# Two-layer decoder on one core: layer-norm rows moved to ScalarE, statistics in one tile, slots routing in half steps

## The chip, the core and the metric

The kernel runs on one core of one Trainium2 chip. The metric is the device time of one execution in microseconds, as a median of runs. A core has a TensorE (PE; its weight loads are listed as PEld), a VectorE (DVE), a ScalarE (ACT), a GpSimd (POOL) and a SyncE (SP) that issues most DMAs. Each engine works through its own queue in the order in which the program's scheduler put the instructions.

## What is computed

`x` is 64 sequences (batches) of 128 rows by 256 columns in f32, `ctx` likewise, and `mask` says which rows of a batch are valid. Every step adds to `x` a function of its layer norm:

```python
x = x + L0_attn(ln(x))              # windowed attention, 7 neighbours, 16 heads of 16
x = x + L0_xattn(ln(x), ctx, mask)  # cross attention: (softmax(q k / 4) sm v Wp + bp) * mask
x = x + L0_ffn(ln(x))               # 64 slots: gelu router, top 8, GRU update of the slots
x = x + L1_attn(ln(x))              # causal self-attention with a bias per head (fire)
x = x + L1_xattn(ln(x), ctx)        # cross attention, no mask
x = x + L1_ffn(ln(x))               # quantized linear, depthwise convolution, silu, linear
```

`ln(x)` is `(x - mean) / sqrt(var + 1e-5)` over the columns, without weights. In the first cross attention both the probabilities and the output are multiplied by the row's mask.

## The kernel before

The 64 batches are worked on in 16 groups of `GB` = 4. `x` passes through DRAM between stages; within a stage `Flow.reach(g)` issues the loads of the groups up to g on SP and `Flow.store` writes finished ones back. The stages in the order of time are called A to F here: A window attention (`stage_window`), B the cross attention of layer 0 with the slots feed-forward layer woven in (`stage_cross0`, `Slots`), then the tail of that stage, in which only slots work is left (`slots.finish()`), D self-attention (`stage_attn` with `cross=False` and a bias), E the second cross attention (`stage_attn` with `cross=True`), F the quantized feed-forward layer.

**The layer norm.** `ln_stats` (lines 126 to 137) takes mean and variance of four batches on VectorE (L133, L134), adds 1e-5 (L135, tile `ln_ve`), and raises to the power −0.5 on POOL (L136, `ln_rs`). It has four small tiles: `ln_st`, `ln_mv`, `ln_ve`, `ln_rs`. `layernorm` (L140) then makes the normalized rows on VectorE, one instruction of 128x256 for each batch (L143). Stage A makes its rows on ScalarE instead, by `scaled_rows` (L260): `nm = -mean * rs` on VectorE, then `rs * x + nm` for each batch (L265). `transpose_group` turns rows with PE into two PSUM banks, copied out by ScalarE (L159) and VectorE (L161).

**The attention loop.** `attention_stage` (L577) runs B, D and E. Half step j works on batch n = j // 2 and on half hf = j % 2 of its heads, each a burst of up to 32 score matmuls. In one burst lie the first scores `sm` of batch n (their negated row maxima are wanted) and the second scores `se` of the half step j − 3 (transposed, with the maxima already in the query, for the exponentials). Then:

- `score_halves` (L490): in D the bias is added on VectorE to `sm` (L498, `sb`) and to `se` (L504, `e`); ScalarE takes the exponential (L507, in D L505); VectorE takes the negated maxima (L511, `negmax`).
- even half steps: `shift_query` of the batch begun at j − 2 (PE transposes `negmax`, L523; VectorE adds it to the query, L525, `q`), `divide` of j − 6 (L545 to 556: `rec`, its product with the row mask in B at L554, `ao`), then `prep` of the next batch.
- odd half steps: `weigh_values` of j − 5 (L537, copied by ScalarE to `avs`, L542), `turn_output` of j − 7 (L566, `aT`), `finish_batch` of j − 9 (output projection L176, and the residual sum).
- `tick`, if there is one: a piece of other work.

`sm` and `se` have one PSUM buffer each; the tile `ps`, which everything else of PE writes to, has four.

In B, `prep` (from L672) takes the statistics once a group, and for each batch makes the scaled query rows `qp` on VectorE (L691), adds the masked bias of the output projection to `x` (L694), writes the masked values (`va`, ScalarE), transposes `qp` with PE and copies it out twice on ScalarE into `qt` (L704). The `tick` of B is `Slots.tick`: one step of the routing of a group (`slots_route`, a generator whose `yield`s end the steps) and one step of each of two `slots_update` generators for each group that has been routed. The routing of group g starts after its last batch is finished; its rows `c_xn` come from `layernorm`. What is left when the loop has ended is run by `finish()`.

In D and E, `group_project(g)` is a generator of nine steps (rows `xn`, transposes `xnT`, four halves of query and key, L1142 for the values) which `prep` and `tick` advance, one step in each half step, for the group after the one at work.

Of the kernel before, what the change touches and what calls it, by code (L numbers as in the profile page):

```python
# [10 lines left out]
F = mybir.dt.float32  # L11
# [113 lines left out]

def ln_stats(k, pool, g):
    nc = k.nc
    st = pool.tile([S, GB, 6], F, tag="ln_st", name="ln_st")
    mv = pool.tile([S, GB, 2], F, tag="ln_mv", name="ln_mv")
    ve = pool.tile([S, GB], F, tag="ln_ve", name="ln_ve")  # L130
    rs = pool.tile([S, GB], F, tag="ln_rs", name="ln_rs")
# [3 lines left out]
    nc.vector.tensor_scalar(ve, mv[:, :, 1], 1e-5, None, ALU.add)  # L135
    nc.gpsimd.tensor_tensor(rs, ve, k.expo, ALU.pow)  # L136
    return mv, rs


def layernorm(k, pool, g, out):  # L140
    mv, rs = ln_stats(k, pool, g)
    for b in range(GB):
        k.nc.vector.tensor_scalar(  # L143
            out[:, b, 0:D], k.x[g][:, b, :], mv[:, b, 0:1], rs[:, b : b + 1],
            ALU.subtract, ALU.mult,
        )

# [111 lines left out]

def scaled_rows(k, pool, g, mv, rs, out):  # L260

    nm = pool.tile([S, GB], F, tag="ln_nm", name="ln_nm")
    k.nc.vector.scalar_tensor_tensor(nm, mv[:, :, 0], -1.0, rs, ALU.mult, ALU.mult)
    for b in range(GB):
# [178 lines left out]
class Batch:  # L443
    pass

# [130 lines left out]

def attention_stage(k, pool, w1, prep, wo, lay, bias_s=None, bias_t=None, tick=None):  # L577

# [59 lines left out]
def stage_cross0(k, w, wc):  # L638
# [3 lines left out]
    with k.tc.tile_pool(name="wb", bufs=2) as wp, k.tc.tile_pool(name="wb1", bufs=1) as w1, \  # L642
# [31 lines left out]
        def prep(bi):  # L674
            g, b = divmod(bi, GB)
            if b == 0:
# [5 lines left out]
                nc.vector.tensor_scalar(r4, rs, 0.25, None, ALU.mult)  # L682
                stats[g] = mv, r4
            mv, r4 = stats[g]
            mk = w.mask[:, bi : bi + 1]
            if b == GB - 1 and g + 1 < k.G:
# [7 lines left out]
            nc.vector.scalar_tensor_tensor(xb, w.bp, mk, xb, ALU.mult, ALU.add)  # L694
            cv = cxs[g][:, b, :].rearrange("p (h d) -> p h d", d=DH)
# [3 lines left out]
            t.kt = kts[g % 2][:, :, b * S : (b + 1) * S]  # L699
            p = psum(k)  # L700
            for c in range(2):
                nc.tensor.transpose(p[:, c * S : (c + 1) * S], qp[:, c * 128 : (c + 1) * 128], k.ident)
            for par in range(2):
                nc.scalar.activation(  # L704
                    t.qt[:, par::2], p[:, 0 : 2 * S].rearrange("p (c l) -> p c l", l=S), AF.Identity,
                    scale=w.par[:, par : par + 1], bias=w.row[:, par : par + 1],
                )
            t.va, t.row_scale = va, mk

            def fin(y):  # L710
                nc.vector.scalar_tensor_tensor(xb, y, mk, xb, ALU.mult, ALU.add)

            t.fin = fin
# [18 lines left out]
def prep_cross0(k, pool):  # L732
# [3 lines left out]
    w.bp = load_row(k, pool, "b_bp")  # L736
    w.mask = load(k, pool, "mask")
    w.par = pool.tile([128, 2], F, name="b_par")
    w.row = pool.tile([128, 2], F, name="b_row")
# [351 lines left out]
def stage_attn(k, w, cross, bias=None):  # L1091
# [3 lines left out]
    with k.tc.tile_pool(name=pre, bufs=2) as wp, k.tc.tile_pool(name=pre + "1", bufs=1) as w1:  # L1095
# [8 lines left out]
        def group_project(g):  # L1104

            xn = w1.tile([S, GB, D], F, tag="xn", name="xn")
            kvT = None
            if cross:
                kvT = wp.tile([128, 2, GB * S], F, tag="kvT", name="kvT")
                nc.sync.dma_start(out=kvT, in_=k.a["ctxT"][g])  # L1110
            k.flow.reach(g + 1)
            layernorm(k, wp, g, xn)
            nc.vector.tensor_tensor(
                k.x[g], k.x[g], w.bvo.unsqueeze(1).to_broadcast([S, GB, D]), ALU.add
            )
# [3 lines left out]
            if not cross:  # L1119
                kvT = xnT  # L1120
            yield
# [33 lines left out]
        def advance(g, parts):  # L1155
            for _ in range(parts):
                if g in pending and next(pending[g], pending) is pending:
                    del pending[g]

        def prep(bi):  # L1160
            g, b = divmod(bi, GB)
            if bi == 0:
                pending[0] = group_project(0)
# [8 lines left out]
            t.va, t.row_scale = va[:, b], None  # L1172
            xb = k.x[g][:, b, :]
# [442 lines left out]
```

## Time and profile before

| | us |
|---|---|
| median of three runs | 3199.1 (3198.59 to 3200.51) |
| the profiled execution, its own time | 3198.04 |
| its span in the trace | 3196.2 |
| PE busy in the span | 2756.9 (86%) |
| VectorE busy | 2457.0 (77%) |
| ScalarE busy | 1464.5 (46%) |
| POOL busy | 460.1 (14%) |
| mean granted clock of TensorE | 0.927 |

A row of the profile's tables reads: line of the kernel, engine, operation, the tile written and the tiles read, shape and count; then busy time and the mean of one in ns, and the idle time of the engine just before such instructions with what ended most of it. A timeline row starts with the start in us and the duration; in brackets stands the idle time before it and its releaser. A row of the table of windows gives, for a stretch of the span, its length, the busy time (and instructions) of PE, PEld, DVE, ACT and POOL, the granted clock of TensorE as a share of full speed, the share of the DMA engines that is busy and GB/s. A busy PE is not PE at full speed: the records lengthen when the granted clock is low.

The chain that ended last belongs to PE for 52% of the span and to VectorE for 35%. A score matmul takes 295 ns in the mean (6144 rows of `sm`, 514.1 us), `negmax` 1219 ns, the exponential 1022 ns, `q` 681 ns.

### The profile page before, as it was taken

To read this page: it belongs to the slowest core of one execution; us is meant where nothing else is said; L and a number is where in the kernel's file an instruction comes from. 1 tells how busy PE (TensorE), PEld (TensorE's weight loads), DVE (VectorE), ACT (ScalarE), POOL (GpSimd) and SP (SyncE) were. 2 spreads that over 40 slices of the span, in tenths; PEclk is the share of its full clock that TensorE was granted. 3 is DMA by queue.
4 is the path that set the end of the run, shared out by engine and by line. 5 is a ranking of instruction groups with operands and counts; after the bars stand their busy time and mean duration, and the time that the engine had idled before them with its cause. 6 is when DMAs were issued, how large, how long until landed. Compare 5 with 4: busy or idle time off the path is not lost.

```text
span 3196.2 us, 63468 instructions
## 1 busy us (share of the span) xinstructions
PE 2756.9 (86%) x26850; PEld 1801.7 (56%) x26876; DVE 2457.0 (77%) x4818; ACT 1464.5 (46%) x2395; POOL 460.1 (14%) x360
## 2 busy tenths in 40 slices
PE   5859988688888888888888988979999998888887
PEld 2324433466666666556666666657667775343343
DVE  7967988787777777778888888865655555899997
ACT  3222221264554554434434444435555555766664
POOL 6555764100000000010000000020000000100000
PEclk9968998799999999989989998989999999999998
DMA  4100111211111111000000000011111111010000
GB/s 150 53 16 27 40 40 40 74 37 45 52 42 45 52 35 35 27 29 15 28 28 28 15 28 28 28 47 35 54 41 41 48 48 41 14 35 32 33 20 27
DMA packets 60011, 123.82 MB, mean 39 GB/s; under 512 B 9088, under 2 KB 34064, under 8 KB 59472
## 3 DMA queue, kind: packets, MB, share of 16 engines
q1 hardware_dynamic: 59168, 118.28, 10.8%
q8 instruction: 212, 3.47, 0.4%
q0 software_dynamic: 560, 1.49, 0.2%
q14 instruction: 71, 0.58, 0.1%
HBM read 77.76 MB, written 41.98 MB: 37 GB/s over the span
## 4 chain that ended last, share of the span: by engine, by line
PE 52%; DVE 35%; ACT 4%; issue 4%; POOL 3%; DMA 1%; SPq 0%; DVEq 0%; POOLq 0%; ACTq 0%
PE ps L176 9%; PE ps L167 8%; PE sm L484 8%; PE ps L537 6%; PE se L484 5%; DVE negmax L511 5%; DVE e L504 3%; PE cv L1316 3%; PE ps L1142 3%; DVE hs L1370 2%; DVE pv L372 2%; PE ps L566 2%; DVE hp L1306 2%; DVE oT L376 2%; PE sc L366 1%
## 5 line engine op out<-in xcount | busy, mean ns | idle before, releaser
L484 PE MATMUL sm<-kt,qt 32*128 32x128 f32 x6144 | 514.1, 295 | 113.3 <-DVE negmax L511 95.7
L484 PEld LDWEIGHTS sm<-kt,qt 32*128 32x128 f32 x6144 | 422.2, 192 | 287.1 <-DVE negmax L511 112.4
L484 PE MATMUL se<-q,kt 32*128 32x128 f32 x6144 | 469.2, 292 | 44.7 <-DVE q L525 41.6
L511 DVE TENSOR_REDUCE negmax<-sm 128x8 f32<-128x1024 f32 x256 | 312.0, 1219 | 200.4 <-PE se L484 190.5
L484 PEld LDWEIGHTS se<-q,kt 32*128 32x128 f32 x6144 | 394.1, 194 | 77.5 <-DVE q L525 47.3
L507 ACT ACTIVATE e<-se 128x1024 f32<-128x1024 f32 x256 | 261.6, 1022 | 204.6 <-PE se L484 201.3
L136 POOL TENSOR_TENSOR ln_rs<-ln_ve,expo 128x4 f32<-128x4 f32 x96 | 100.6, 1048 | 1410.5 <-DVE ln_ve L135 1230.8
L1316 PE MATMUL cv<-hp,taps 128*128 128x512 f32 x480 | 241.3, 639 | 35.8 <-DVE hp L1306 35.5
L314 POOL TENSOR_TENSOR pr<-pad,qt 128x896 f32<-128x896 f32 x128 | 247.1, 1953 | 140.6 <-PE s L326 97.2
L505 ACT ACTIVATE e<-e 128x1024 f32<-128x1024 f32 x128 | 135.3, 1057 | 210.4 <-DVE e L504 210.3
L498 DVE TENSOR_TENSOR sb<-sm,bias_s 128x1024 f32<-128x1024 f32 x128 | 153.9, 1202 | 85.8 <-PE se L484 82.0
L542 ACT COPY avs<-ps 128x512 f32<-128x512 f32 x192 | 112.2, 585 | 146.0 <-PE ps L537 145.8
L1316 PEld LDWEIGHTS cv<-hp,taps 128*128 128x128 f32 x480 | 93.3, 203 | 140.4 <-issue 84.0
L372 DVE TENSOR_TENSOR pv<-sc,pad 128x896 f32<-128x896 f32 x128 | 137.8, 1081 | 40.3 <-PE sc L366 40.3
L504 DVE TENSOR_TENSOR e<-se,bias_t 128x1024 f32<-128x1024 f32 x128 | 155.6, 1215 | 3.2 <-PE se L484 1.8
L511 DVE TENSOR_REDUCE negmax<-sb 128x8 f32<-128x1024 f32 x128 | 154.9, 1210 | 0.5
L133 DVE BATCH_NORM_STATS2 ln_st<-x 128x6 f32<-128x256 f32 x384 | 147.6, 427 | 4.4 <-DMA x<-in_x_dram 1.7
L376 DVE TENSOR_REDUCE oT<-pv 128x128 f32<-128x896 f32 x128 | 136.7, 1072 | 1.3
L366 PE MATMUL sc<-fw,spread 32*128 32x448 f32 x512 | 103.5, 649 | 33.4 <-DVE pv L372 28.8
L525 DVE TENSOR_TENSOR q<-ps,qt 128x512 f32<-128x512 f32 x192 | 130.7, 681 | 1.0 <-PE ps L523 1.0
L1176 DVE TENSOR_TENSOR x<-ps,x 128x256 f32<-128x256 f32 x128 | 53.9, 421 | 91.2 <-PE ps L176 91.2
L549 PE MATMUL ps<-ident,avs 128*128 128x128 f32 x768 | 115.5, 273 | 0.7 <-ACT avs L542 0.7
(329 smaller groups left out, 5657.4 us busy)
## 6 DMA issues: line engine op xcount, KB each, us to landing
x<-in_x_dram SPq DMA_DIRECT2D x16, 512.0 KB
ab<-x SPq DMA_DIRECT2D x16, 512.0 KB
x<-ab SPq DMA_DIRECT2D x16, 512.0 KB
cx<-in_ctx_dram SPq DMA_DIRECT2D x16, 512.0 KB
kt<-in_ctxT_dram SPq DMA_DIRECT2D x128, 64.0 KB
cd<-x SPq DMA_DIRECT2D x16, 512.0 KB
x<-cd SPq DMA_DIRECT2D x16, 512.0 KB
de<-x SPq DMA_DIRECT2D x16, 512.0 KB
```

The source lines that it names most:

```text
L167: k.nc.tensor.matmul(out, w[:, kc, c0 : c0 + cn], rhsT[:, kc, n0 : n0 + n], start=(kc == 0), stop=(kc == 1),)
L176: k.nc.tensor.matmul(out, aT[:, kc, :], w[:, kc, :], start=(kc == 0), stop=(kc == 1))
L314: k.nc.gpsimd.tensor_tensor(pr[:, c], shift_windows(t.kt, b, c), t.qt[:, c, b, :].unsqueeze(1).to_broadcast([128, WIN, S]), ALU.mult,)
L372: nc.vector.tensor_tensor(pv, bc[th][:, :, 0 : WIN * 64].rearrange("p c (l w) -> p c l w", w=WIN), shift_windows2(t.vt, b, th), ALU.mult,)
L376: nc.vector.tensor_reduce(oT[:, :, 64 * th : 64 * th + 64], pv, AX.X, ALU.add)
L484: k.nc.tensor.matmul(ts[side][:, rr, c * S : (c + 1) * S], st[rows, c, :], mv[rows, c, :], start=True, stop=True,)
L498: nc.vector.tensor_tensor(sb, src, bias_s[:, hf * 2 : hf * 2 + 2, :], ALU.add)
L504: nc.vector.tensor_tensor(e, est, bias_t[:, hf * 2 : hf * 2 + 2, :], ALU.add)
L507: nc.scalar.activation(e, est, AF.Exp)
L511: nc.vector.tensor_reduce(b.lay.extra(b.nm, hf * 2), src.rearrange("p r (c m) -> p r c m", m=S), AX.X, ALU.max, negate=True,)
L537: nc.tensor.matmul(av[32 * r : 32 * r + 32, c * S : (c + 1) * S], b.va[:, b.lay.head(c, r), :], b.e[r // 2][:, r % 2, c * S : (c + 1) * S] ...
L1316: nc.tensor.matmul(pc, w.taps[:, CONV_PE.index(j), t, :], hp[:, :, t : t + S], start=(t == 0), stop=(t == 2),)
```

## The change

1. *One tile of statistics a group.* `ln_stats` keeps everything in one tile `ln` of ten rows.
2. *Rows on ScalarE.* In B (`qp`), in the slots routing (`c_xn`), and in D and E (`xn`), the normalized rows are made on ScalarE by `activation(Identity, scale, bias)` with `nm` from the new `row_bias`. `layernorm` is gone. D and E also copy both halves of `xnT` on ScalarE.
3. *Slots rows in two half steps.* `slots_route` makes `c_xn` in two steps of two batches each, so it has two `yield`s more.
4. *B's order.* The masked bias, the transposes of `qp` and `qt` become `more()`, called at the end of the odd half step. The output is finished at a lag of 8 half steps instead of 9, ahead of the other parts of its half step. The two factors of the mask (on `rec` and on the output) become one factor `mask * mask` in `fin`.
5. *D's order.* With a bias, `shift_query` stands between the burst and `score_halves`, where it stood behind them.
6. *Groups of D and E begin earlier.* `begin(g + 2)` at the end of the odd half step ahead of a group's first batch; the statistics are the step that `begin` runs, the rows another. The output bias is added to `x` after the transposes. `kvT` (the context in E) has three buffers.

```diff
 def ln_stats(k, pool, g):
+    ln = pool.tile([S, 10, GB], F, tag="ln", name="ln")
+    st = ln[:, 0:6].rearrange("p i b -> p b i")
+    mv = ln[:, 6:8].rearrange("p i b -> p b i")
+    ve, rs = ln[:, 8], ln[:, 9]
...
-def scaled_rows(k, pool, g, mv, rs, out):
+def row_bias(k, pool, mv, rs):
     nm = pool.tile([S, GB], F, tag="ln_nm", name="ln_nm")
     k.nc.vector.scalar_tensor_tensor(nm, mv[:, :, 0], -1.0, rs, ALU.mult, ALU.mult)
-    for b in range(GB):
+    return nm
+
+def scaled_rows(k, pool, g, mv, rs, out, nm=None, bs=range(GB)):
+    if nm is None:
+        nm = row_bias(k, pool, mv, rs)
+    for b in bs:
...
 def divide(k, pool, b):
-    if b.row_scale is not None:
-        nc.vector.tensor_scalar(rec, rec, b.row_scale, None, ALU.mult)
...
 def attention_stage(..., tick=None, lag=9):
+    early = bias_s is not None
     start(0)
+    if bs[0].more:
+        bs[0].more()
...
             ts = score_burst(k, first, second)
+            if early and at(j, 2):
+                shift_query(k, pool, at(j, 2))
             score_halves(k, pool, w1, ts, first, second, bias_s, bias_t)
+        if lag % 2 == hf and at(j, lag):
+            finish_batch(k, bs.pop((j - lag) // 2), wo)
         if hf == 0:
-            if at(j, 2):
+            if not early and at(j, 2):
                 shift_query(k, pool, at(j, 2))
...
-            if at(j, 9):
-                finish_batch(k, bs.pop((j - 9) // 2), wo)
+            if n + 1 < k.NB and bs[n + 1].more:
+                bs[n + 1].more()
...
 # stage_cross0, prep
-                stats[g] = mv, r4
+                stats[g] = r4, row_bias(k, wp, mv, r4)
...
-            nc.vector.tensor_scalar(
-                qp, xb, mv[:, b, 0:1], r4[:, b : b + 1], ALU.subtract, ALU.mult,
+            nc.scalar.activation(
+                qp, xb, AF.Identity, scale=r4[:, b : b + 1], bias=nm[:, b : b + 1]
             )
...
-        attention_stage(k, wp, w1, prep, w.wp, Heads(True), tick=slots.tick)
+        attention_stage(k, wp, w1, prep, w.wp, Heads(True), tick=slots.tick, lag=8)
...
 def slots_route(k, w, g, wp, w1):
-    layernorm(k, wp, g, xn)
-    yield
+    mv, rs = ln_stats(k, wp, g)
+    yield
+    nm = row_bias(k, wp, mv, rs)
+    for half in range(2):
+        scaled_rows(k, wp, g, mv, rs, xn, nm, range(2 * half, 2 * half + 2))
+        yield
...
 # stage_attn, group_project
-            xn = w1.tile([S, GB, D], F, tag="xn", name="xn")
...
-                kvT = wp.tile([128, 2, GB * S], F, tag="kvT", name="kvT")
+                kvT = wp.tile([128, 2, GB * S], F, tag="kvT", name="kvT", bufs=3)
...
-            layernorm(k, wp, g, xn)
+            mv, rs = ln_stats(k, w1, g)
+            yield
+            xn = w1.tile([S, GB, D], F, tag="xn", name="xn")
+            scaled_rows(k, wp, g, mv, rs, xn)
+            yield
+            xnT = w1.tile([128, 2, GB * S], F, tag="xnT", name="xnT")
...
+                nc.scalar.copy(xnT[:, kc, :], p)
...
             nc.vector.tensor_tensor(
                 k.x[g], k.x[g], w.bvo.unsqueeze(1).to_broadcast([S, GB, D]), ALU.add
             )
-            yield
-            xnT = w1.tile([128, 2, GB * S], F, tag="xnT", name="xnT")
-            transpose_group(k, xn, xnT)
...
 # stage_attn, prep and tick
+        def begin(g):
+            if g < k.G and g not in pending:
+                pending[g] = group_project(g)
+                advance(g, 1)
...
-                if g + 1 < k.G:
-                    pending[g + 1] = group_project(g + 1)
+                begin(g + 1)
...
-                advance((j // 2 + 1) // GB + 1, 1)
+                g, b = divmod(j // 2 + 1, GB)
+                advance(g + 1, 1)
+                if b == GB - 1:
+                    begin(g + 2)
```

More of the change, by code (lines that the diff above doesn't have):

```diff
@@ L127, in ln_stats @@
     nc = k.nc
[L128 to L131, printed above, removed]
+    ln = pool.tile([S, 10, GB], F, tag="ln", name="ln")
+    st = ln[:, 0:6].rearrange("p i b -> p b i")
+    mv = ln[:, 6:8].rearrange("p i b -> p b i")
+    ve, rs = ln[:, 8], ln[:, 9]
     for b in range(GB):
@@ L137, in ln_stats @@
     return mv, rs
-def layernorm(k, pool, g, out):
-    mv, rs = ln_stats(k, pool, g)
-    for b in range(GB):
[L143 to L146, printed above, removed]
 def transpose_group(k, src, dst):
@@ L257, in prep_window @@
     return w
-def scaled_rows(k, pool, g, mv, rs, out):
+def row_bias(k, pool, mv, rs):
     nm = pool.tile([S, GB], F, tag="ln_nm", name="ln_nm")
     k.nc.vector.scalar_tensor_tensor(nm, mv[:, :, 0], -1.0, rs, ALU.mult, ALU.mult)
-    for b in range(GB):
+    return nm
[3 more added lines that the diff above has]
+    for b in bs:
         k.nc.scalar.activation(
@@ L443 @@
 class Batch:
-    pass
+    more = None
 class Heads:
@@ L574, in finish_batch, with attention_stage @@
     b.fin(py[:, 0:D])
-def attention_stage(k, pool, w1, prep, wo, lay, bias_s=None, bias_t=None, tick=None):
+def attention_stage(k, pool, w1, prep, wo, lay, bias_s=None, bias_t=None, tick=None, lag=9):
     nms = []
@@ L682, in prep @@
                 nc.vector.tensor_scalar(r4, rs, 0.25, None, ALU.mult)
-                stats[g] = mv, r4
-            mv, r4 = stats[g]
+                stats[g] = r4, row_bias(k, wp, mv, r4)
+            r4, nm = stats[g]
             mk = w.mask[:, bi : bi + 1]
@@ L690, in prep @@
             qp = wp.tile([S, D], F, tag="qp", name="qp")
-            nc.vector.tensor_scalar(
-                qp, xb, mv[:, b, 0:1], r4[:, b : b + 1], ALU.subtract, ALU.mult,
+            nc.scalar.activation(
+                qp, xb, AF.Identity, scale=r4[:, b : b + 1], bias=nm[:, b : b + 1]
             )
-            nc.vector.scalar_tensor_tensor(xb, w.bp, mk, xb, ALU.mult, ALU.add)
             cv = cxs[g][:, b, :].rearrange("p (h d) -> p h d", d=DH)
@@ L699, in prep, with more, fin @@
             t.kt = kts[g % 2][:, :, b * S : (b + 1) * S]
[L700 to L706, printed above, removed]
-                )
[L708 to L713, printed above, removed]
+            t.va = va
+            def more():
+                nc.vector.scalar_tensor_tensor(xb, w.bp, mk, xb, ALU.mult, ALU.add)
+                p = psum(k)
+                for c in range(2):
+                    nc.tensor.transpose(
+                        p[:, c * S : (c + 1) * S], qp[:, c * 128 : (c + 1) * 128], k.ident
+                    )
+                for par in range(2):
+                    nc.scalar.activation(
+                        t.qt[:, par::2], p[:, 0 : 2 * S].rearrange("p (c l) -> p c l", l=S),
+                        AF.Identity, scale=w.par[:, par : par + 1], bias=w.row[:, par : par + 1],
+                    )
+            def fin(y):
+                nc.vector.scalar_tensor_tensor(
+                    xb, y, w.mask2[:, bi : bi + 1], xb, ALU.mult, ALU.add
+                )
+            t.more, t.fin = more, fin
             return t
         slots = Slots(k, wc, c2, w1)
-        attention_stage(k, wp, w1, prep, w.wp, Heads(True), tick=slots.tick)
+        attention_stage(k, wp, w1, prep, w.wp, Heads(True), tick=slots.tick, lag=8)
         slots.finish()
@@ L737, in prep_cross0 @@
     w.mask = load(k, pool, "mask")
+    w.mask2 = pool.tile([S, k.NB], F, name="mask2")
+    nc.vector.tensor_tensor(w.mask2, w.mask, w.mask, ALU.mult)
     w.par = pool.tile([128, 2], F, name="b_par")
@@ L1104, in group_project @@
         def group_project(g):
-            xn = w1.tile([S, GB, D], F, tag="xn", name="xn")
             kvT = None
             if cross:
-                kvT = wp.tile([128, 2, GB * S], F, tag="kvT", name="kvT")
+                kvT = wp.tile([128, 2, GB * S], F, tag="kvT", name="kvT", bufs=3)
                 nc.sync.dma_start(out=kvT, in_=k.a["ctxT"][g])
             k.flow.reach(g + 1)
-            layernorm(k, wp, g, xn)
+            mv, rs = ln_stats(k, w1, g)
[4 more added lines that the diff above has]
+            xnT = w1.tile([128, 2, GB * S], F, tag="xnT", name="xnT")
+            for kc in range(2):
+                p = psum(k)
+                for b in range(GB):
+                    nc.tensor.transpose(
+                        p[:, b * S : (b + 1) * S], xn[:, b, kc * 128 : (kc + 1) * 128], k.ident
+                    )
+                nc.scalar.copy(xnT[:, kc, :], p)
+            if not cross:
+                kvT = xnT
             nc.vector.tensor_tensor(
@@ L1115, in group_project @@
             )
-            yield
-            xnT = w1.tile([128, 2, GB * S], F, tag="xnT", name="xnT")
-            transpose_group(k, xn, xnT)
-            if not cross:
-                kvT = xnT
             yield
@@ L1162, in prep @@
             if bi == 0:
-                pending[0] = group_project(0)
+                begin(0)
             if b == 0:
                 advance(g, 9)
-                if g + 1 < k.G:
-                    pending[g + 1] = group_project(g + 1)
+                begin(g + 1)
             advance(g + 1, 1)
@@ L1171, in prep @@
             t.qt, t.kt = qt[:, :, b * S : (b + 1) * S], kt[:, :, b * S : (b + 1) * S]
-            t.va, t.row_scale = va[:, b], None
+            t.va = va[:, b]
             xb = k.x[g][:, b, :]
```

## The prediction

> **What bounds the kernel now.** I read the table of windows first, cut at the six stages (A window attention, B cross attention of layer 0 with the slots routing between its steps, then B's tail of slots work, D self-attention with bias, E cross attention of layer 1, F bitnet).
>
> ```profile
> core 0: us, PE busy (x) PEld busy (x) DVE busy (x) ACT busy (x) POOL busy (x), PEclk, DMA share, GB/s
> 0.00:593.00 593.00, 471.43 (x2104) 208.73 (x2104) 481.85 (x748) 138.59 (x238) 341.98 (x220) 0.87 0.16 53
> 593.00:1303.00 710.00, 624.12 (x7792) 480.92 (x7792) 542.53 (x1492) 373.68 (x635) 29.76 (x42) 0.92 0.14 44
> 1303.00:1401.00 98.00, 77.35 (x418) 48.92 (x418) 62.39 (x204) 35.68 (x62) 10.79 (x13) 0.86 0.12 41
> 1401.00:2143.00 742.00, 650.64 (x7571) 477.70 (x7570) 610.89 (x881) 309.43 (x466) 30.74 (x41) 0.94 0.07 26
> 2143.00:2690.00 547.00, 526.71 (x7385) 382.89 (x7385) 316.85 (x561) 285.86 (x444) 12.08 (x12) 0.99 0.13 43
> 2690.00:3196.20 506.20, 406.69 (x1594) 202.53 (x1616) 442.45 (x936) 321.25 (x552) 34.71 (x32) 0.93 0.08 29
> ```
>
> PE is busy 86 to 88% of B and D and 96% of E; ScalarE is half idle in all three. VectorE holds 76% of B and 82% of D. So B and D are two engines handing work back and forth, E is PE alone. The spacing of equal rows gives the steady group of four batches: B 47.8 us, D 44.1, E 35.1. In B the timeline of VectorE shows what one group loses at its seam:
>
> ```profile
> 1019.91 0.17 DVE L135 TENSOR_SCALAR ln_ve<-ln_mv 128x4 f32<-128x4 f32 x1
> 1021.27 1.38 DVE L143 TENSOR_SCALAR c_xn<-x,ln_mv,ln_rs 128x256 f32<-128x256 f32 x4 [1.19 <-POOL ln_rs L136]
> 1022.57 1.22 DVE L511 TENSOR_REDUCE negmax<-sm 128x8 f32<-128x1024 f32 x1
> 1023.71 0.68 DVE L525 TENSOR_TENSOR q<-ps,qt 128x512 f32<-128x512 f32 x1
> ```
>
> negmax, which the next burst needs, stands behind a wait of 1.19 us for POOL's power and four c_xn rows (1.38). PE then stands still for 2.71 us, and the windows show what follows: 0.16 us of work, then half clock.
>
> ```profile
> 1022.00:1024.00 2.00, 0.16 (x2) 0.16 (x2) 2.00 (x5) 0.24 (x1) 0.00 (x0) 0.92 0.00 0
> 1024.00:1026.00 2.00, 2.00 (x11) 1.77 (x12) 1.94 (x10) 0.07 (x1) 0.00 (x0) 0.50 0.00 0
> 1026.00:1028.00 2.00, 2.00 (x16) 1.67 (x16) 0.36 (x1) 0.99 (x2) 0.00 (x0) 0.50 0.00 0
> ```
>
> It lasts 6.8 us (1023.7 to 1030.5), 3.4 us of PE's work, in every steady group. In D the timeline of PE shows the other loss, a score burst cut in two by the shifted query:
>
> ```profile
> 1723.13 1.16 PE L484 MATMUL sm<-kt,qt 32*128 32x128 f32 x16
> 1724.86 1.16 PE L484 MATMUL se<-q,kt 32*128 32x128 f32 x16 [0.57 <-DVE q L525]
> ```
>
> Sixteen rows alone take 1.16 us; all 32 interleaved take 1.17 (2392.01 to 2393.19 in E). A cut costs 1.16, and 0.57 of waiting where q is late. In the issue order of the old kernel every odd burst of D is cut; in the new one a quarter, since shift_query goes ahead of the score halves and q no longer stands behind sb, e and negmax of the next step.
>
> **Part by part.** The sum is made against the profiled execution (3198.0 us; span 3196.2), which is 1.1 below the median of 3199.1.
>
> *A, one tile of statistics:* the next group's statistics wait for the whole tile, and nm follows the power at once, so VectorE may wait for POOL there; on POOL's queue the power now stands behind two pr (L314, 1.95 us each). A steady wait has the row above, 1.19 us; 16 groups give 0 to +19, and earlier statistics could give −5. PE (79%) and VectorE (81%) alternate and hide part: **+5**.
>
> *B, ScalarE rows.* Off VectorE per group: four c_xn (0.409 each), four qp (0.363), four products of rec and mask (0.225, L554): 4.0 of a sum of 43.1. Onto ScalarE: eight rows of 0.597 (L265): 27.6 becomes 32.4 of 47.8, so there is room. On the path goes only the seam: 1.19 + 1.38 = 2.57 us ahead of negmax, and the 3.4 us of clock behind it. Two nm (0.17) lie in waits; mask squared is one operation ahead of the stage.
>
> *B, "more".* bp's addition, two transposes and two qt (L704, 0.56 each on ScalarE) move from the even half step to the end of the odd one. Now the next burst needs qt, which stands behind exp, avs and aT on ScalarE. The trace has no such wait. Its ends: 0, where slots work on PE (pieces of 0.75 to 1.8 us) lies between, and transposes 0.27 + exp 1.02 + qt 1.12 = 2.4 us a batch. With exp half done I take 1.4; in the issue order one batch in six has no piece: 4/6 × 1.4 = +0.9 a group. finish a half step earlier (lag 8) puts q behind x (0.42, L1176) in places; PE has the transposes there: 0, at worst 4 × 0.4 a group. Sum −2.6 − 3.4 + 0.9 = −5.0 a group, × 13 steady groups = **−65** (ends −110, all seams and 3.5 of VectorE's 4.0 gone, and +96, below).
>
> *Half steps of slots.* c_xn takes two further ticks: a group's routing takes 9 where there are 8 half steps a group. It falls behind, and one group more is left after the last burst. The tail writes x at 1333.10, 1355.97 and 1378.17, 22.5 apart: **+22.5** (ends 0, if D's projection begins beside it, and +45).
>
> *D.* Per pair of half steps 12.0, 10.41, 10.42, 11.3. Three whole bursts instead of cut ones bring about 1.0 each in two pairs and 0.8 in the others (of 1.73: the rest goes where VectorE is the limit). xn (4 × 0.409) and the xnT copy (0.687) leave VectorE in the last pair; nm and its wait (0.17 + 1.19) come in the first: 12.6, 9.4, 9.4, 8.2 = 39.6. Behind the waiting nm stand the next sb, e and negmax on VectorE, and PE's burst waits for these. A second way: VectorE's sum of 41.3 − 2.3 + 0.2 + 1.2 waiting = 40.4. I take 40.4: −3.7 × 15 = **−56** (ends −100, when the half-clock stretches go as well: windows at 0.5 or less add up to 96 us of D, 48 of work; and −20, if each group gets a new one like B's, 3.4 us of work, a third of it hidden). Here ScalarE's rows lie in its 55% of idle time; without it they would cost 3.1 a group.
>
> *E.* The same move takes out one PE wait of 1.17 + 0.21 us a group, and half the groups show half clock after it:
>
> ```profile
> 2420.00:2422.00 2.00, 0.68 (x3) 0.29 (x2) 2.00 (x8) 0.00 (x0) 0.00 (x0) 1.00 0.78 260
> 2424.00:2426.00 2.00, 2.00 (x28) 1.48 (x17) 1.16 (x2) 1.20 (x3) 0.00 (x0) 0.50 0.00 0
> ```
>
> Together up to 2.2 us a group; exp now stands behind the rows (2.4 us), covered by transposes, avs and Wq on PE. I take 1.6 × 15 = **−24** (0 to −33). Groups begin a half step earlier: the x and context loads move up on SP, past the stores of the group before, and the third context buffer keeps them from waiting for the last reader; at a DMA share of 0.13 I cost that at 0 and, uncovered, one load a group. F changes only in order: **0** (±6).
>
> Sum: 5 − 65 + 22.5 − 56 − 24 = −117: **3081 us**.
>
> *A rule beside the row.* The Trainium skill, "TensorE: Matmul & The Clock Gate", Part 1, says that the array's clock halves after at least one idle window of about 3.4 us, counted freely. This trace differs: the half clock in B follows 2.71 us of idling, in E 1.38. By the page such gaps cost no clock, the 3.4 us a group would have another cause and stay, and the sum would be the first rival's time; the measurement decides against it as far as 13 alike groups can.
>
> **Rivals.**
> 1. *The clock loss stays.* If the half clock after the seam goes with the group's load and not with the idle 2.71 us, B gains 1.6 a group: −21 in place of −65, 3125 us. Against it: it begins right behind the gap, every 47.8 us. For it: dips in A and F without that seam.
> 2. *qt eats B's gain.* At 1.4 us in nearly every batch (+4.7 more a group) B stands still: 3146 us. For it: ScalarE's queue before qt is exp, avs, aT.
> 3. *Slower.* In B the stalls ahead of the burst come in every batch (4 × 1.4) and two of four are long enough to halve the clock (2 × 3.4): −5.0 + 12.4 = +7.4 a group, +96: 3198 − 52.5 + 96 = 3242 us. It decides from +4.0 a group, where D's and E's gains are used up. E's 1.38 us of idling shows that short gaps can do it; against it speaks slots work on PE in five batches of six.
> 4. *D doesn't do what it says:* q comes late, as the sb of the next step waits for its burst and q for the transposes; bursts interleave but wait 1 us longer. D unchanged: 3137 us. For it: q is late by 0.57 us already now; against it: the transposes stand ahead of sb in the new issue order.
> 5. *More goes than I count:* with VectorE's cuts the half-clock stretches of B (89 us) and D go too. For it: most start behind a PE wait for VectorE; against it: E's 1.38 us shows how little it takes. D to −100, B to −110, E to −33: 3198 + 27.5 − 243 = 2982 us.
>
> **Numbers.** Forecast 0.45, rivals 0.15, 0.12, 0.10, 0.09, 0.09. Leaving out the slower case and most of the last gives 2990 to 3170. Faster by over 0.2% (6.4 us, about what a measurement of this kernel can tell) 0.88, within it 0.02, slower 0.10.
>
> **What would show it.** Right: no half clock every group in B, group 42 to 44; negmax with no c_xn ahead; D groups near 40 with three of four odd bursts whole; a wait of about 1.2 us for the power ahead of nm; a tail of about 120 us; E below 34. Wrong: PE waits for ScalarE's qt ahead of most of B's bursts, D at 44 with PE waiting for q, a tail still near 98, or A longer by over 15 us.

## The result, and the profile after

The changed kernel takes 3181.4 us (median of 4 runs, 3176.8 to 3183.7) against 3198.9 of before: a ratio of 0.9942, 95% interval 0.9925 to 0.996. It is faster, as forecast, but by 0.6%: the medians differ by 18 us in place of the forecast 117. The forecast of 3081 us and its range (2990 to 3170) are both missed.

To compare stages I cut both traces at the same events: A ends with the first row maxima of B, then come the last of B, the first of D, the first of E and the last of E. The half-clock column adds the time at a granted clock of 0.5 or less (in brackets: stretches), the idle column the time without a PE row.

| stage | before | after | change | forecast | half clock before, after | PE idle before, after |
|---|---|---|---|---|---|---|
| A | 598.5 | 617.6 | +19.1 | +5 | 165 (17), 177 (19) | 123.8, 133.3 |
| B | 704.4 | 669.2 | −35.2 | −65 | 104 (13), 90 (14) | 83.6, 69.7 |
| tail | 100.7 | 133.5 | +32.8 | +22.5 | 27 (4), 41 (7) | 20.9, 26.2 |
| D | 739.1 | 687.3 | −51.8 | −56 | 96 (18), 75 (14) | 91.1, 65.2 |
| E | 542.2 | 554.6 | +12.4 | −24 | 10 (3), 31 (9) | 20.2, 23.5 |
| F | 511.1 | 512.6 | +1.5 | 0 | 66 (13), 68 (14) | 99.6, 97.8 |

The changes sum to −21.2 us; the profiled spans (3196.2 and 3174.8) differ by 21.4, the rest is rounding. The table of windows of the changed kernel, with these cuts:

```profile
core 0: us, PE busy (x) PEld busy (x) DVE busy (x) ACT busy (x) POOL busy (x), PEclk, DMA share, GB/s
0.00:617.60 617.60, 484.31 (x2124) 215.22 (x2124) 493.34 (x775) 142.57 (x246) 343.46 (x222) 0.86 0.16 53
617.60:1286.90 669.30, 599.57 (x7702) 457.88 (x7703) 473.54 (x1244) 412.62 (x727) 28.53 (x39) 0.93 0.14 43
1286.90:1420.30 133.40, 107.26 (x509) 66.38 (x507) 73.41 (x244) 58.27 (x106) 8.96 (x13) 0.85 0.12 41
1420.30:2107.60 687.30, 622.09 (x7550) 446.76 (x7550) 581.61 (x816) 341.84 (x541) 30.75 (x41) 0.95 0.08 29
2107.60:2662.20 554.60, 531.14 (x7313) 378.08 (x7314) 285.40 (x517) 319.68 (x511) 13.09 (x13) 0.97 0.12 40
```

VectorE lost 102 us of busy time over the whole span (2457.0 to 2355.3) and ScalarE gained 135, as intended; the span followed by a fifth of that. The first hint of where the rest went is what VectorE now waits for. Some of its waits over the whole changed kernel (total, times, longest):

```profile
DVE ln_nm L256 <- POOL ln L138: 89.1, 61, 9.2
DVE x L709 <- ACT qp L698: 80.1, 36, 4.9
DVE x L1147 <- ACT xn L265: 68.1, 18, 7.9
```

nm waits for POOL's power. That wait is not new, but it has grown: ahead of everything that uses the power, VectorE waited 67 us in the kernel before and waits 104 now. The last two are new kinds of wait: the masked bias of B, added to `x` in place, waits until ScalarE has read that `x` for qp; the output bias of D and E waits for ScalarE's xn in the same way. E shows most plainly what such a wait does. VectorE at a seam of the changed E:

```profile
2240.90 1.23 DVE L511 TENSOR_REDUCE negmax<-sm 128x8 f32<-128x1024 f32 x1 [0.56 <-PE se L484]
2245.80 1.22 DVE L1147 TENSOR_TENSOR x<-x,e_bvo 128x1024 f32<-128x1024 f32 x1 [3.68 <-ACT xn L265]
2246.94 1.22 DVE L511 TENSOR_REDUCE negmax<-sm 128x8 f32<-128x1024 f32 x1
```

and ScalarE beside it:

```profile
2242.73 1.07 ACT L1144 COPY xnT<-ps 128x512 f32<-128x512 f32 x2
2243.69 2.08 ACT L265 ACTIVATE xn<-x,ln_nm,ln 128x256 f32<-128x256 f32 x4
```

The burst that this negmax reads ends at 2244.24. VectorE is idle then, but the next in its queue is the bias, which waits until the fourth row of xn ends at 2245.77 and then takes 1.22 us. negmax starts 2.7 us after its data were there, and PE waits for it 1.46 us where it waited 1.17 before. In the kernel before, VectorE has the rows, the same bias and the averages there, with no wait between them:

```profile
2417.29 1.37 DVE L143 TENSOR_SCALAR xn<-x,ln_mv,ln_rs 128x256 f32<-128x256 f32 x4
2418.69 1.23 DVE L1113 TENSOR_TENSOR x<-x,e_bvo 128x1024 f32<-128x1024 f32 x1
2419.84 0.37 DVE L134 BATCH_NORM_AGGREGATE ln_mv<-ln_st 128x2 f32<-128x6 f32 x4
2420.13 1.19 DVE L511 TENSOR_REDUCE negmax<-sm 128x8 f32<-128x1024 f32 x1
```

The xn that left VectorE (1.37 us) was replaced by a wait of 1.5 us for the same xn on ScalarE (2244.24 to 2245.77), and the bias's own 1.22 us stayed. In the changed kernel half clock follows:

```profile
2248.00:2250.00 2.00, 1.58 (x32) 1.30 (x32) 2.00 (x8) 1.15 (x2) 0.00 (x0) 1.00 0.00 0
2250.00:2252.00 2.00, 2.00 (x11) 1.17 (x12) 1.04 (x6) 1.21 (x2) 0.75 (x1) 0.54 0.00 0
```

### The profile page after: what moved, and what is told of

Its sections match the earlier page's. It is cut to its first block, busy times and chain, and to the rows that moved or that the text cites. A ratio compares the mean times of both kernels' runs of the same rounds, so it can differ in the third digit from the quotient of the medians.

```text
span 3174.8 us, 63554 instructions
## 1 busy us (share of the span) xinstructions
PE 2759.1 (87%) x26876; PEld 1769.7 (56%) x26876; DVE 2355.3 (74%) x4531; ACT 1599.2 (50%) x2683; POOL 459.3 (14%) x360
## 4 chain that ended last, share of the span: by engine, by line
PE 48%; DVE 35%; ACT 9%; POOL 4%; issue 2%; DMA 2%; SPq 0%; POOLq 0%; DVEq 0%; ACTq 0%
PE ps L169 9%; PE sm L484 8%; PE ps L160 8%; PE se L484 4%; PE ps L537 4%; DVE negmax L511 3%; PE ps L1171 3%; DVE sb L498 3%; DVE e L504 3%; PE cv L1352 3%; DVE pv L372 2%; DVE hs L1406 2%; DVE oT L376 2%; DVE hp L1342 2%; DVE ln L135 2%
## 5 line engine op out<-in xcount | busy, mean ns | idle before, releaser
L484 PE MATMUL sm<-kt,qt 32*128 32x128 f32 x6144 | 539.3, 297 | 69.2 <-DVE negmax L511 40.2
L484 PEld LDWEIGHTS sm<-kt,qt 32*128 32x128 f32 x6144 | 436.4, 192 | 240.6 <-DVE negmax L511 71.8
L484 PE MATMUL se<-q,kt 32*128 32x128 f32 x6144 | 481.0, 292 | 56.5 <-DVE e L504 25.8
L484 PEld LDWEIGHTS se<-q,kt 32*128 32x128 f32 x6144 | 402.4, 192 | 84.1 <-issue 37.4
L138 POOL TENSOR_TENSOR ln<-ln,expo 128x4 f32<-128x4 f32 x96 | 98.4, 1025 | 1676.2 <-DVE ln L137 1158.8
L314 POOL TENSOR_TENSOR pr<-pad,qt 128x896 f32<-128x896 f32 x128 | 248.4, 1964 | 137.7 <-PE s L326 97.8
L135 DVE BATCH_NORM_STATS2 ln<-x 128x6 f32<-128x256 f32 x384 | 148.8, 406 | 10.9 <-DMA x<-ab 10.5
L265 ACT ACTIVATE xn<-x,ln_nm,ln 128x256 f32<-128x256 f32 x192 | 100.3, 595 | 31.4 <-DVE ln_nm L256 24.7
```

The costliest lines, as they stand in the source:

```text
L314: k.nc.gpsimd.tensor_tensor(pr[:, c], shift_windows(t.kt, b, c), t.qt[:, c, b, :].unsqueeze(1).to_broadcast([128, WIN, S]), ALU.mult,)
L484: k.nc.tensor.matmul(ts[side][:, rr, c * S : (c + 1) * S], st[rows, c, :], mv[rows, c, :], start=True, stop=True,)
```

## The experiments

The theory (theory 1 in the expectations): rows that went to ScalarE turned later operations of VectorE into waits for ScalarE, and these stand at the head of VectorE's queue, ahead of the row maxima that PE needs; with the wait of nm for POOL they ate the gain. The rival: ScalarE's own longer queue delays exp and qt, and VectorE's idle time is only where that shows. A third suspect for A alone was the one tile of statistics.

Each run's stages were cut as above; times in us. The last column is the median of the run's timings, not the profiled span. The kernel before, timed beside each run, had medians of 3198.9 to 3208.8, so that a total is read to about 10 us unless its ratio is given; stages come from the traces, one profiled execution of each run.

| run | A | B | tail | D | E | time |
|---|---|---|---|---|---|---|
| before | 598.5 | 704.4 | 100.7 | 739.1 | 542.2 | 3198.9 |
| changed | 617.6 | 669.2 | 133.5 | 687.3 | 554.6 | 3181.4 |
| x1 four tiles | 603.7 | 671.8 | 131.1 | 654.5 | 558.4 | 3133.7 |
| x2 bias off VectorE's queue | 616.9 | 665.0 | 135.6 | 661.5 | 551.0 | 3141.5 |
| x3 x2 and two buffers | 622.5 | 668.4 | 136.2 | 660.5 | 547.4 | 3149.5 |
| x4 slots rows in one step | 622.4 | 717.9 | 98.9 | 692.5 | 558.3 | 3202.1 |
| x5 x1 and x2 | 606.0 | 661.6 | 132.9 | 650.6 | 524.2 | 3089.4 |
| x6 order undone | 621.2 | 648.8 | 133.6 | 735.3 | 554.5 | 3208.1 |
| x7 x5, E's rows on VectorE | 602.1 | 668.1 | 132.1 | 650.8 | 578.6 | 3148.8 |
| x8 x5, nm on POOL | 598.1 | 667.7 | 133.3 | 654.4 | 526.8 | 3093.1 |
| x9 x5, qt early again | 603.9 | 639.7 | 133.2 | 651.2 | 524.3 | 3068.3 |
| x10 x9, eight half steps | 606.2 | 660.5 | 109.6 | 651.2 | 524.3 | 3060.1 |
| x11 before, one tile alone | 616.8 | 708.0 | 100.6 | 739.2 | 548.1 | 3228.6 |
| x12 before, early query alone | 599.9 | 704.4 | 100.7 | 691.4 | 542.2 | 3152.7 |

Runs whose code is the same in a stage still differ there by up to 6 us in A (the changed kernel, x2 and x3: 616.9 to 622.5) and by 6.5 in B (x5 and x7); in D (x5, x7, x9, x10) and E (x5, x9, x10) by under 1. Differences below that are not read.

### x1: four tiles of statistics again

```diff
 def ln_stats(k, pool, g):
-    ln = pool.tile([S, 10, GB], F, tag="ln", name="ln")
...
+    st = pool.tile([S, GB, 6], F, tag="ln_st", name="ln_st")
+    mv = pool.tile([S, GB, 2], F, tag="ln_mv", name="ln_mv")
+    ve = pool.tile([S, GB], F, tag="ln_ve", name="ln_ve")
+    rs = pool.tile([S, GB], F, tag="ln_rs", name="ln_rs")
```

> The changed kernel with the four small tiles of statistics of before (everything else as changed). Stage A took 598.5 us before and 617.6 after (start to the first negmax of B). If the one tile is what costs A its 19 us, since nm then waits for the power right behind the statistics (1.13 us and more a group), A comes back to 598 to 603. If A lost them to something else (order of weight preparation, clock), it stays above 612. D (687) and E (555) are expected within 5 us of the changed kernel by the first theory, as the waits for ScalarE's rows that I hold responsible there do not come from this tile.

A came back to 603.7, about as expected, but D fell by 33 us, which I had not expected. In the changed D the statistics of a group run in one piece, and nm waits at the end of it:

```profile
1672.39 0.31 DVE L136 BATCH_NORM_AGGREGATE ln<-ln 128x2 f32<-128x6 f32 x2
1672.73 0.17 DVE L137 TENSOR_SCALAR ln<-ln 128x4 f32<-128x4 f32 x1
1674.11 0.16 DVE L256 SCALAR_TENSOR_TENSOR ln_nm<-ln 128x4 f32<-128x4 f32 x1 [1.21 <-POOL ln L138]
1674.19 1.22 DVE L498 TENSOR_TENSOR sb<-sm,bias_s 128x1024 f32<-128x1024 f32 x1
1675.32 0.68 DVE L525 TENSOR_TENSOR q<-ps,qt 128x512 f32<-128x512 f32 x1
```

With four tiles the scheduler lays the parts of two groups over each other: nm of one group stands ahead of the averages of the next, so its power is long done, and no bracket appears.

```profile
1642.13 0.15 DVE L256 SCALAR_TENSOR_TENSOR ln_nm<-ln_mv,ln_rs 128x4 f32<-128x4 f32 x1
...
1645.92 0.37 DVE L136 BATCH_NORM_AGGREGATE ln_mv<-ln_st 128x2 f32<-128x6 f32 x4
1646.33 0.17 DVE L137 TENSOR_SCALAR ln_ve<-ln_mv 128x4 f32<-128x4 f32 x1
1646.40 1.40 DVE L135 BATCH_NORM_STATS2 ln_st<-x 128x6 f32<-128x256 f32 x4
```

PE's wait for sb in D falls with it. First the changed kernel, then x1:

```profile
PE sm L484 <- DVE sb L498: 24.8, 18, 1.7
```

```profile
PE sm L484 <- DVE sb L498: 6.5, 14, 1.6
```

### x11: the one tile alone, in the kernel before

The same edit turned round: the kernel before with the tile `ln` in place of the four.

> The kernel before with the one tile of statistics alone. If one tile keeps the scheduler from spreading a group's statistics over time (its parts can't belong to two groups at once), A 598 becomes 610 to 620, and D (739) and E (542), where VectorE's rows then follow the power at once, grow by 1.2 us a group, 10 to 25 each; the kernel is slower than before by 30 to 60 in all. Rival (the tile costs only where nm follows it on VectorE and ScalarE reads it): A as above, B, D and E within 6 of before.

3228.6 us, a ratio to before of 1.0079 (1.0059 to 1.0099): slower. A 616.8 is the changed kernel's A, so the tile is all of A's 19 us; VectorE's wait ahead of nm in A is 29.3 us in both, against 15.2 before. D did not move, E grew by 6, and B's 4 are within what equal code shows: neither of the two expectations as a whole. So D pays for the tile only together with other parts of the change. The trace above points to nm on VectorE behind the power; no run has the one tile in the changed kernel with nm elsewhere.

### x2 and x3: the biases out of VectorE's queue

```diff
 # group_project (D and E)
-            nc.vector.tensor_tensor(
+            nc.gpsimd.tensor_tensor(
                 k.x[g], k.x[g], w.bvo.unsqueeze(1).to_broadcast([S, GB, D]), ALU.add
 # prep of B
             def more():
-                nc.vector.scalar_tensor_tensor(xb, w.bp, mk, xb, ALU.mult, ALU.add)
...
             def fin(y):
...
+                nc.vector.scalar_tensor_tensor(xb, w.bp, mk, xb, ALU.mult, ALU.add)
 # x3 in addition
-            mv, rs = ln_stats(k, w1, g)
+            mv, rs = ln_stats(k, wp, g)
```

> The changed kernel with the in-place bias additions taken out of VectorE's way: in D and E the output bias is added by POOL, in B the masked bias is added in fin, behind the output. In the changed kernel VectorE stands 80 us in B ahead of the masked bias until ScalarE has made qp, and 68 us in D and E ahead of the output bias until ScalarE has made xn; the row maxima wait behind. Theory 1 (these in-place waits ate the gain): B 669 becomes 640 to 650, D 687 becomes 665 to 680. E 555 comes down less than it could, to 535 to 550, since the next statistics then take the same place and wait for the rows too, through their one buffer. Rival (ScalarE's longer queue itself delays exp and qt, and VectorE's idle time is only where it shows): B and E within 5 us of the changed kernel.

> As the run before, with two buffers of the tile of statistics in D and E in place of one, so that the next group's statistics need not wait for the rows of this one. Theory 1: E 515 to 525 us (the PE idle time of 1.46 + 0.21 us a group gone, 27 us, and the half clock after it), D as in the run before. Rival (exp late behind four rows of 0.597): the PE idle time at E's seam stays and E is above 545.

D fell by 26. B's 4 are within what equal code shows, although its 80 us of waiting were gone, and for B theory 1 falls: VectorE waits for PE's scores ahead of negmax instead (32 us in the changed B, 84 in x2), so that wait lay beside PE's work. E fell by 4 and 7 only. By their numbers B and E of x2 and E of x3 came out as the rival had it (within 5 us, and above 545); x5 decides between the two for E. In x2 the statistics had taken the bias's place in the queue, as foreseen; the second buffer of x3 did not cure it. x2, then x3:

```profile
DVE ln L135 <- ACT xn L265: 61.8, 19, 7.0
```

```profile
DVE ln L135 <- ACT xn L265: 42.0, 14, 3.7
```

The scheduler moved the statistics of x3 one group further ahead, into the new buffer (when the rows of a group begin, the statistics of three groups have begun, of two in x2), and the next ones wait again for rows that read their tile.

### x5: four tiles and biases off the queue

The edits of x1 and x2 together.

> Both edits at once: four tiles of statistics, the output bias of D and E on POOL, the masked bias of B in fin. In the changed kernel and in the three runs with one of the edits, something on VectorE waits for ScalarE's xn ahead of E's row maxima (the bias, or the statistics that the scheduler moved into its place). With both nothing is left there. Theory 1 (head of VectorE's queue): E 555 becomes 515 to 530, with half clock near 0; D 640 to 650; A about 603; total 3075 to 3095. Rival (exp behind four rows of ScalarE is the late one): E stays at 545 or more and only D moves.

E 524.2, as theory 1 had it, PE idle 23.5 to 9.2, half clock 31 us (9 stretches) to 7 (1); D 650.6 with 20 us of half clock in 2 stretches, from 75 in 14. The total of 3089.4 is a ratio to before of 0.9624 (0.9592 to 0.9657). The windows of D and E in this run:

```profile
1400.50:2051.10 650.60, 603.10 (x7545) 432.62 (x7546) 562.39 (x800) 344.63 (x544) 67.99 (x57) 0.98 0.08 30
2051.10:2575.30 524.20, 515.03 (x7318) 368.50 (x7322) 265.88 (x489) 320.74 (x511) 45.68 (x27) 0.99 0.12 43
```

At E's seam nothing stands ahead of the maxima any more; negmax waits for PE, not the other way round. VectorE, and ScalarE's rows at the same seam:

```profile
2253.28 1.22 DVE L511 TENSOR_REDUCE negmax<-sm 128x8 f32<-128x1024 f32 x1 [2.16 <-PE se L484]
2254.42 0.68 DVE L525 TENSOR_TENSOR q<-ps,qt 128x512 f32<-128x512 f32 x1
```

```profile
2252.68 2.08 ACT L265 ACTIVATE xn<-x,ln_nm,ln_rs 128x256 f32<-128x256 f32 x4
2254.66 1.01 ACT L507 ACTIVATE e<-se 128x1024 f32<-128x1024 f32 x1
```

So theory 1 holds for E. The two ScalarE-facing waits on VectorE stood in for one another; taking away either alone brought 4 us or less, both brought 30. The rival, that exp is late behind xn's rows, is out for E: exp stands behind the same four rows here. What the runs do not separate is the bias's wait from its own 1.22 us, since x2 and x5 take both off VectorE. In D the two edits overlap as well: four tiles bring 33 us with the bias on VectorE (x1), 11 with it on POOL (x2 to x5).

### x7: E's rows on VectorE, in x5

```diff
+            if cross:
+                for b in range(GB):
+                    nc.vector.tensor_scalar(
+                        xn[:, b], k.x[g][:, b, :], mv[:, b, 0:1], rs[:, b : b + 1], ALU.subtract, ALU.mult,
+                    )
+            else:
+                scaled_rows(k, wp, g, mv, rs, xn)
```

> The run with both edits, and in E alone the rows xn on VectorE again, as before. If moving E's rows to ScalarE has a worth of its own, once no wait stands ahead of the row maxima, E is 10 to 25 us longer than in the run with both edits (1.6 us of VectorE at the seam of each group, idle PE and half clock after it). If it hasn't, E is the same within 4 us.

E is 54 us longer than in x5, with 37.1 us of PE idle and 55 of half clock in 12 stretches. The direction is as expected, the size is twice the upper end, and longer than before's E (542.2). The trace shows what now stands ahead of negmax. With the rows on VectorE, POOL's bias starts as soon as they end, and the addition of 1e-5 (`ln_ve`), 0.17 us elsewhere, takes 2.00 us beside it and ends when the bias ends, in all 13 groups that have it.

```profile
2276.85 2.35 POOL L1153 TENSOR_TENSOR x<-x,e_bvo 128x1024 f32<-128x1024 f32 x1 [34.83 <-DVE xn L1137]
```

```profile
2277.22 2.00 DVE L137 TENSOR_SCALAR ln_ve<-ln_mv 128x4 f32<-128x4 f32 x1
2279.14 1.39 DVE L135 BATCH_NORM_STATS2 ln_st<-x 128x6 f32<-128x256 f32 x4
2280.46 1.20 DVE L511 TENSOR_REDUCE negmax<-sm 128x8 f32<-128x1024 f32 x1
```

With the statistics also ahead of negmax, VectorE takes 5.07 us there from the start of xn to negmax (2275.39 to 2280.46), against 2.84 in the kernel before. So x7 measures this order too, and not what ScalarE's rows alone are worth.

### x4: the slots rows in one half step

```diff
     mv, rs = ln_stats(k, wp, g)
-    yield
     nm = row_bias(k, wp, mv, rs)
-    for half in range(2):
-        scaled_rows(k, wp, g, mv, rs, xn, nm, range(2 * half, 2 * half + 2))
-        yield
+    scaled_rows(k, wp, g, mv, rs, xn, nm)
+    yield
```

> The changed kernel with the slots rows made in one half step, together with their statistics, so that a group's routing takes as many half steps as before. The tail took 100.7 us before and 133.5 after. Theory: the tail is back to 100 to 112, and B (669) grows by 0 to 15 for the work that it keeps; total 15 to 30 below the changed kernel. Rival (the tail grew because each step in it became slower, waits for POOL and ScalarE): the tail stays above 125.

The tail is back at 98.9, so it is the two added half steps that lengthen it, by 34.6 us. But B grew by 48.7, more than three times the upper end, and its steady group stood at 47.6, as if nothing had been changed. B and tail together are 14 longer than in the changed kernel. The wait for negmax went as predicted (PE's idle time ahead of sm in B's groups of the window 800 to 1260: 52.8 us before, 4.3 here), but another came in that window and half clock rose to 127 us in 24 stretches:

```profile
PE se L484 <- ACT e L507: 29.9, 12, 2.7
```

In each steady group exp stands on ScalarE behind the four slots rows, and these behind nm. ScalarE, then PE:

```profile
863.73 2.07 ACT L265 ACTIVATE c_xn<-x,ln_nm,ln 128x256 f32<-128x256 f32 x4 [0.82 <-DVE ln_nm L256]
865.71 1.00 ACT L507 ACTIVATE e<-se 128x1024 f32<-128x1024 f32 x1
```

```profile
866.76 0.49 PE L484 MATMUL se<-q,kt 32*128 32x128 f32 x4 [2.69 <-ACT e L507]
```

The seam's 2.71 us of PE waiting for negmax became 2.69 us of PE waiting for exp. So the rival, ScalarE's longer queue delaying exp, which x5 rules out for E, holds in x4's B, and in part in the changed kernel's.

### x6: the two changes of order undone

```diff
-    early = bias_s is not None
+    early = False
...
             if n + 1 < k.NB:
                 start(n + 1)
+                if bs[n + 1].more:
+                    bs[n + 1].more()
...
-            if n + 1 < k.NB and bs[n + 1].more:
-                bs[n + 1].more()
```

> The changed kernel with its two changes of order undone: in D shift_query is again behind the score halves, in B the transposes of qp and qt come again in the even half step (finish stays at a lag of 8). By the prediction's step for D (three cut bursts a group made whole are worth about 3.6 us a group) D 687 becomes 735 to 750. By the rival (bursts of D are not the limit, VectorE is) D stays within 15 us. For B the prediction's cost of the late qt was 0.9 us a group: B 669 becomes 655 to 665 if so, and 690 or more if the new order is what B gained by.

D goes to 735.3, as expected: the early query is worth 48 us. B goes down to 648.8: the deferred qt costs 20 us, more than the 12 that I had put on it (0.9 in each of 13 groups). It does not show as PE's waits for qt (3.3 us in the changed B) nor as idle time or half clock (69.7 and 90 us there, 71.3 and 97 here). The 4032 score rows of B are on PE for 204.0 us in the changed kernel and for 185.5 here, and the rows change less often between `sm` and `se` there (2909 times, 3235 here): the bursts are less interleaved.

### x12: the early query alone, in the kernel before

```diff
             ts = score_burst(k, first, second)
+            if bias_s is not None and at(j, 2):
+                shift_query(k, pool, at(j, 2))
             score_halves(k, pool, w1, ts, first, second, bias_s, bias_t)
         if hf == 0:
-            if at(j, 2):
+            if bias_s is None and at(j, 2):
```

> The kernel before with D's early shift_query alone. By the prediction's step, cut bursts made whole bring 0.8 to 1.0 us in each of four pairs: D 739 becomes 675 to 695. If VectorE's xn and xnT at the group's end must leave as well for that to come through, D is 705 to 725. All other stages are within 5 of before.

D 691.4, −47.7, as expected, the other stages unmoved; 3152.7 us in all, a ratio to before of 0.9838 (0.9821 to 0.9856). This one edit alone beats the whole change (0.9942). PE's waits in D, before:

```profile
PE se L484 <- DVE q L525: 38.9, 43, 1.7
```

and in x12 (the wait for q is nearly gone, and one for e, which now stands behind q, has come):

```profile
PE se L484 <- DVE e L504: 24.7, 35, 0.9
...
PE se L484 <- DVE q L525: 0.8, 1, 0.8
```

### x8: nm on POOL, in x5

```diff
-    k.nc.vector.scalar_tensor_tensor(nm, mv[:, :, 0], -1.0, rs, ALU.mult, ALU.mult)
+    k.nc.gpsimd.tensor_tensor(nm, mv[:, :, 0], rs, ALU.mult)
+    k.nc.gpsimd.tensor_scalar(nm, nm, -1.0, None, ALU.mult)
```

> The run with both edits, and nm made by POOL (a product and a change of sign) right behind its power, so that VectorE never waits for POOL. The changed kernel's VectorE waits 89 us ahead of nm for the power, with four tiles 41. Theory (those waits lie on the path in A and D): A 603 becomes 595 to 600 and D 5 to 15 shorter. Rival (they lie beside PE): no stage moves by over 4 us, or A is longer, since POOL's queue holds pr.

A 598.1 against 606.0, D and E 4 and 3 longer, B 6 longer, the time 3093.1 against 3089.4. A lies 4 to 8 us below the four runs with x5's A (602.1 to 606.2), little more than equal code differs by, and there is no gain in all: once the tiles are four, the wait for the power is not what holds D and E.

### x9 and x10: the version that the runs point to

x9 is x5 with `more()` called where it was in x6; D keeps its early query. x10 joins the last two steps of the routing:

```diff
     nc.scalar.activation(e, e, AF.Exp)
-    yield
     nc.vector.tensor_tensor(al, al, e, ALU.mult)
```

> The run with both edits, and B's transposes of qp and qt again in the even half step, as before the change; D keeps its early shift_query. If the deferred qt costs what the run with the order undone showed (B 669 to 649), B 662 becomes 636 to 648 and the total 3066 to 3078. If that gain came only from the waits for qp that this kernel no longer has ahead of the row maxima, B stays above 655.

> The run before this, with the last two steps of the slots routing joined, so that a group takes eight half steps, as many as there are, and the two half steps of rows stay. If the tail is longer because routing falls behind by one half step a group, the tail 133 becomes 98 to 112, and B grows by less than that, 5 to 25, for the slots work of about one group more: total 3045 to 3075. Rival (the shorter tail is paid in full in B, as with the rows in one step): B 685 or more, no gain.

x9: B 639.7 and 3068.3 us, both as expected, a ratio to before of 0.9564 (0.9548 to 0.958). x10: the tail fell by 23.6, B grew by 20.8, both within what was expected, and the time is 3060.1, a ratio of 0.9535 (0.952 to 0.955). Tail and B together are only 3 us shorter. The shorter tail is thus paid nearly in full in B, as the rival had it, though not to its 685: this is slots work that moves between the two, and B hides hardly any of it.

## Why the prediction was wrong

The sum over the stages was −117, and −21 was measured. The sign was right; the sum failed in A, in B with its tail, and in E, and D came out near only by cancelling.

1. **A, +5 forecast, +19 measured.** The mechanism was named (nm waits for the power, 0 to +19) and the value taken was too low. x11 shows that the tile alone makes all of it. VectorE's wait ahead of nm grew by 14 us, PE's idle time by 9.5 and half clock by 11, in one execution each.
2. **B and tail, −42.5 forecast, −2.4 measured.** The step that failed is "On the path goes only the seam", with ScalarE's rows put at nothing because "there is room". The wait of the seam did go, but others came in its place. PE's waits in the whole of B, before and then changed:

```profile
PE sm L484 <- DVE negmax L511: 79.9, 58, 3.0
PE se L484 <- ACT e L507: 1.5, 2, 1.2
```

```profile
PE se L484 <- ACT e L507: 21.6, 15, 3.8
PE sm L484 <- DVE negmax L511: 19.7, 12, 4.6
PE ps L953 <- DVE x L723: 11.7, 5, 2.4
```

Of the 21.6 us, 14.7 stand where exp is behind four slots rows on ScalarE. Room in ScalarE's sum says nothing of the place in its queue. With the order undone (x6) the waits for exp are 6.6 us and those for negmax 41.1, so the order decides where this idle time stands. The wait for `x`, the residual sum of the output, is new as well; no run puts the lag of 8 back, so its cause stays open. PE's idle time in B fell by 14 us, half clock only from 104 to 90 us, so of some 44 us of clock (13 × 3.4) 7 came. Before, all 13 stretches of half clock begin behind the seam's wait of 2.7 us; in the changed kernel 11 of 14 begin within 3 us after another PE wait of 1.8 us or more (for exp, for this `x`, for negmax). That is not the first rival: the clock loss did not stay on without a gap, new gaps brought it. The deferred qt is mis-sized too: 20 us (x6) and 22 (x9 against x5) in place of 12. So is the tail: 34.6 (x4) in place of 22.5. Of B's 35 us, 14 are idle time, 7 clock, and the remaining 14 are PE's busy time; 70 of its 7772 rows in B moved to the tail.
3. **D, −56 forecast, −52 measured, right only by cancelling.** The early query alone brings 47.7 (x12). With the query, the rows and four tiles D is 84.6 shorter than before (x1), where the sum without nm and its wait has about 76. The one tile costs 33 of that again, where the sum has 20 (0.17 + 1.19 us in 15 groups). That PE's burst waits in turn was said; what it costs was sized by nm's wait alone. Against x1 the changed D has 19 us more of PE idle time (65.2 and 45.8) and 27 more of half clock (75 and 48), which is 14 us of work.
4. **E, −24 forecast, +12 measured.** The step that failed is "The same move takes out one PE wait of 1.17 + 0.21 us a group". I followed xn from VectorE to ScalarE and asked what waits behind it on ScalarE, exp, which was rightly found to be covered. I did not ask what on VectorE must wait for ScalarE now. The bias is added in place to the `x` that xn reads. On one engine their order cost nothing; on two it is a wait, and it stood ahead of negmax. With it and the one tile's equal wait away (x5), E gains 18 against before: near the 24 of the forecast, though x5 also takes the bias's 1.22 us a group off VectorE, which the forecast did not have. The clock part of the term was misread as well: "half the groups show half clock after it", but in the trace before it is 3 of the 13 groups with this wait, 10 us in all.

Of the rivals, the third (slower), the fourth (D unchanged) and the fifth (more goes than counted) did not come about; the second (qt) did in part, at 20 us. None of them held the wait for ScalarE at the head of VectorE's queue, which cost E its gain, or exp behind the slots rows, which took part of B's.

**The clock.** In the changed E eight of the nine stretches of half clock begin behind PE waits of 1.45 or 1.46 and 0.21 us; 13 groups have these waits, so not each is followed by one. With the wait gone (x5) a single stretch is left. The Trainium skill, "TensorE: Matmul & The Clock Gate", Part 1, gives at least one idle window of about 3.4 us as the condition; the measurement differs, as it did before the change. In B the amount of half clock does not follow the sum of PE's idle time: 90 us with 69.7 us idle in the changed kernel, 127 with 72.9 in x4, 83 with 63.3 in x5, 80 with 80.1 in x10. What decides it is open.

**Left open.** No run undoes the lag of 8, the single mask factor, or the earlier beginning of the groups of D and E. What E's rows on ScalarE are worth with the bias left on VectorE, but behind negmax, was not tried.

## What to carry to other kernels

When a row moves to another engine, look at every later instruction of the old engine that overwrites what the row reads, or the tile that holds its scale: what was free order in one queue becomes a wait for the new engine, and it matters where that wait stands in the old queue. Look as well at what the row now stands ahead of in the new queue: an engine that is half idle can still make the next burst wait. One tile for several small results ties their lifetimes together; a scheduler that reorders can no longer lay two groups over each other, and that cost D 33 us of 687, or 11 with the bias on POOL. Where two waits can take each other's place, removing either alone shows almost nothing (4 us or nothing in E), and only both together show the 30.

## What was not expected of the hardware

Half clock in B rose from 90 us in 14 stretches to 127 in 24 while PE's idle time hardly changed (69.7 to 72.9 us, x4): the sum of the idle time does not tell it. A second buffer took only a third off a wait, since the scheduler filled it at once by running one group further ahead (61.8 us of waiting became 42.0, E 551.0 became 547.4). And an addition of 128x4 on VectorE took 2.00 us in place of 0.17 while POOL added 128x1024 beside it (x7).
